# A software-pipelined attention pass: maxima ahead of statistics, the normalised stream a step later, POOL's sums in another order

## The chip, the core and the metric

The kernel runs on one core of a Trainium2 chip. A core has a matrix engine (PE), a vector engine (DVE), an activation engine (ACT), a general engine (POOL) and a queue engine (SP) that issues DMAs. Each engine works through its own instructions in order, and waits on semaphores for the others. PE writes to PSUM, eight banks of 128 partitions by 512 floats; DVE and ACT read them. The metric is the time of one execution on the device in microseconds; lower is better.

## What is computed

A batch of 16 images of 64 x 64 positions with 128 channels goes through a two-dimensional recurrence, an attention layer and a one-dimensional recurrence, each added to its input. The change is in the attention layer, which takes the result as 16 sequences of 4096 tokens. Its core, cut to what matters here (8 heads of 16 channels, 64 landmarks):

```
xn = (x - mu) * rsqrt(var + eps) * gamma + beta
q, k, v = split(xn @ w_qkv);  q = q * dh ** -0.5
q_l, k_l = means of q and k over 64 stretches of the sequence
attn1 = softmax(q   @ k_l^T)        # 4096 x 64 per head
attn2 = softmax(q_l @ k_l^T)        # 64 x 64, inverted by iteration
attn3 = softmax(q_l @ k^T)          # 64 x 4096
out = attn1 @ pinv(attn2) @ (attn3 @ v) + conv(v)
x + out @ w_out + b_out
```

What follows it begins with a layer norm of each token and a product with W, whose mean and variance over all tokens are needed: "the normalised stream" below.

## The kernel before

Earlier stages leave the landmarks and the inverses of attn2 in memory. The attention pass then walks over groups of 512 tokens: Q = 8 groups per image, 128 groups in all, and one call of `step(s)` per group. The work on one group is spread over many steps, so that a step handles several groups at once. In the names of `step`, `new` is the group whose q, k and v are projected; `mid`, one image behind, is weighed by attn3 (`weigh`, `weights`, `attend_values`); `first` and `cur`, nearly two images behind, take attn1: `compare` makes the scores, `topmost` reduces them to maxima, `soften` and `softened` make the exponentials, `attend`, `convolve`, `divide`, `add_convolved` and `turn_attended` the output; `third` projects the output and adds the input (`output`, `keep_sum`, which writes at_u and sends it to memory in two DMAs); `fourth` takes the statistics of at_u and its normalisation. `after` is the next group to be transposed. With `start` (q = 0) a step also closes one image: `gather` normalises the sums of attn3 @ v, `turn_split` prepares the shift of the next image's exponentials, `spread_values` applies the inverse.

The order in which every engine meets its instructions is the order in which `step` calls these helpers; it is written out by hand (`tc.manual_schedule`), and nothing reorders it. SP's DMAs follow the same order. `first_step` serves the first 8 steps, `last_step` those after the last group was projected.

PSUM is the scarce thing. The banks 0 to 5 and a pair of two are used several times in a step, and a matmul into a bank waits until the last reader of its former contents is through. Those that matter here:

- bank 5: second block of `compare`'s scores, read by `topmost` (L1088, tile at_cmx), then `project_queries` (L948), then `weigh`;
- banks 0 to 3: keys and values, then `greatest` (L973), the scores of attn3 over the group, read by `keep_greatest` (L977, four reductions on DVE, bank 3 first), then `output` (L1158, bank 3), `turn_top` (L1104, bank 2) and `turn_output` (L909 on at_z, bank 1);
- bank 2 in a start step: `gather` (L1061, L1063), read by DVE's reciprocal and products (L1066, L1069), before `greatest` uses it;
- bank 3 again: `turn_split` (L956) ahead of `greatest` in a start step, and `feed` (L1189).

On DVE the statistics are `measure` (four bn_stats of at_u with their four aggregates, L1170 and L1171) and `measure_feed` (one bn_stats of at_fx, L1197). On ACT `normalise` makes at_z in four pieces (L1183), `keep_output` copies its transpose (L924), `keep_feed` copies the product (L1193) and sends it to memory by one DMA (L1194). On POOL `add_weights` adds the four chunks of the exponentials at_e into at_total (L1042, L1045; three in their own step, the one of chunk 2 at the front of the next), `factors` makes the scale and bias for `normalise` (L32, L33, L1177, L1178), `carry` and `carry_bias` prepare the residual at_T (L899, L903; on ACT L897), `part_top` splits the maxima into bfloat16 parts (L1096 to L1099) and `shift` the image's maxima (L984 to L991, after a reduction on DVE, L982).

Of the kernel before, what the change touches and what calls it, by code (L numbers as in the profile page):

```python
# [796 lines left out]
def attention(nc, tc, t1, gamma, beta, wqkv, ident, mhalf, fixed, xp, rows, qm, km, pinvT, vd, t2, wx, wx_stats, out):  # L797
# [20 lines left out]
    with ExitStack() as ctx:  # L818
# [86 lines left out]
        def turn(a, k):  # L905

            p = bank(k, [P, C, P])
            for c in range(C):
                nc.tensor.transpose(p[:, c, :], a[:, c, :], ident)  # L909
            return p.rearrange("p c n -> p (c n)")  # L910

        def turn_rows(gr):
            gr.px = turn(gr.xh, 4)

        def keep_rows(gr):
            gr.xT = wk.tile([P, GC], F32, tag="xT", name="at_xT", bufs=2)
# [121 lines left out]
        def add_weights(gr, cs, start=False, eng=nc.gpsimd):  # L1038

            e, total = gr.e, gr.im.total  # L1040
            if start:
                eng.tensor_tensor(total, e[:, :, cs[0], :], e[:, :, cs[1], :], ALU.add)  # L1042
                cs = cs[2:]
            for c in cs:
                eng.tensor_tensor(total, total, e[:, :, c, :], ALU.add)  # L1045
# [73 lines left out]
        def softened(gr):  # L1119
            gr.eT = wk.tile([P, NP, GC], F32, tag="eT", name="at_eT")  # L1120
            for n in range(NP):
                nc.scalar.activation(gr.eT[:, n], gr.s[n], AF.Exp)  # L1122
# [78 lines left out]
        def group(s):  # L1201
            b, g = divmod(s, Q)
            return images[b].groups[g] if b in images else None
# [13 lines left out]
        def first_step(s):  # L1217
            new, after = group(s), group(s + 1)
            both = pair()
            project_keys(new, both[:, 0])  # L1220
            project_values(new, both[:, 1])
            keep_keys(new)
            turn_rows(after)
            keep_projected(new)
            project_queries(new)
            keep_rows(after)
            keep_queries(new)
            greatest(new)
            keep_greatest(new)
            if s == Q - 1:  # L1230
                shift(new.im)
            fetch(s)

        def last_step(s):
            b, q = divmod(s, Q)
            mid, was = group(s - Q), group(s - Q - 1)
            first, cur, third, fourth, fifth = (group(s - 2 * Q + d) for d in (1, 0, -1, -2, -3))
            start = q == 0
            if first:
                compare(first)  # L1240
            if cur:
                softened(cur)
            if start and mid:
                fifth = None
                add_weights(was, (2,))
                sums(mid.im)
                measure(fourth)
                factors(fourth)
                turn_split(mid.im)
            if first:  # L1250
                topmost(first)
                carry_factors(first)
                carry(first, 2, nc.gpsimd)
            if start and was:
                gather(was.im)
            if first:
                part_top(first)
                carry(first, 3, nc.gpsimd)
            if third:
                output(third, 0)  # L1260
                keep_sum(third)
                measure(third)
            if fifth:
                feed(fifth, 1)
                keep_feed(fifth)
                measure_feed(fifth)
            if start and was:
                spread_values(was.im)
            if mid:
                weigh(mid)  # L1270
                weights(mid)
            if fourth:
                normalise(fourth)
            if cur:
                attend(cur)
            if mid:
                add_weights(mid, (3, 1, 0), mid.g == 0)
            if cur:
                convolve(cur, pair())
                divide(cur)  # L1280
            if first:
                turn_top(first)
                keep_top(first)
            if cur:
                add_convolved(cur)
            if mid:
                attend_values(mid)
                keep_values(mid)
            if fourth:
                turn_output(fourth, 4)  # L1290
                keep_output(fourth)
            if first:
                carry(first, 0, nc.scalar)
                carry(first, 1, nc.scalar)
                soften(first)
            if third:
                factors(third)
            if first:
                carry_bias(first)
            if cur:  # L1300
                turn_attended(cur)
            if mid:
                add_weights(mid, (2,), eng=nc.vector)
            fetch(s)

        def step(s):
            b, q = divmod(s, Q)
            new, after, mid, was = group(s), group(s + 1), group(s - Q), group(s - Q - 1)
            first, cur, third, fourth = (group(s - 2 * Q + d) for d in (1, 0, -1, -2))
            start = q == 0  # L1310
            if first:
                compare(first)
            if cur:
                softened(cur)
            if fourth:
                measure(fourth)
            if new:
                project_keys(new)
            if was:
                add_weights(was, (2,))  # L1320
            if start and mid:
                sums(mid.im)
            if new:
                project_values(new)
            if first:
                topmost(first)
            if fourth:
                factors(fourth)
            if new:
                keep_keys(new)  # L1330
                project_queries(new)
                keep_projected(new)
            if start and was:
                gather(was.im)
            if start and mid:
                turn_split(mid.im)
            if new:
                keep_queries(new)
                greatest(new)
            if first:  # L1340
                carry_factors(first)
                carry(first, 2, nc.gpsimd)
            if fourth:
                normalise(fourth)
            if mid:
                weigh(mid)
            if new:
                keep_greatest(new)
            if first:
                part_top(first)  # L1350
            if third:
                output(third)
            if mid:
                weights(mid)
            if first:
                carry(first, 3, nc.gpsimd)
            if new and q == Q - 1:
                shift(new.im)
            if start and was:
                spread_values(was.im)  # L1360
            if first:
                turn_top(first)
            if fourth:
                turn_output(fourth)
            if third:
                keep_sum(third)
            if cur:
                attend(cur)
            if fourth:
                keep_output(fourth)  # L1370
            if mid:
                add_weights(mid, (3, 1, 0), mid.g == 0)
            if cur:
                convolve(cur, pair())
                divide(cur)
            if first:
                carry(first, 0, nc.scalar)
            if fourth:
                feed(fourth)
            if first:  # L1380
                keep_top(first)
            if after:
                turn_rows(after)
            if fourth:
                keep_feed(fourth)
            if after:
                keep_rows(after)
            if cur:
                add_convolved(cur)
            if mid:  # L1390
                attend_values(mid)
                keep_values(mid)
            if first:
                soften(first)
                carry(first, 1, nc.scalar)
                carry_bias(first)
            if cur:
                turn_attended(cur)
            if fourth:
                measure_feed(fourth)  # L1400
            fetch(s)

        with tc.manual_schedule(
            engines={mybir.EngineType.PE, mybir.EngineType.DVE, mybir.EngineType.Activation, mybir.EngineType.Pool}
        ):
            projected(images[0])
            for g, a in enumerate(rows):
                group(g).xh = a
            turn_rows(group(0))
            keep_rows(group(0))  # L1410
            for s in range(Q * (B + 2) + 3):
                (first_step if s < Q else step if s < Q * B else last_step)(s)
# [299 lines left out]
```

## Time and profile before

| | us |
|---|---|
| median of 3 runs | 3751.4 |
| lowest, highest run | 3747.28, 3753.3 |
| the profiled execution | 3744.15 |
| its span | 3742.7 |
| attention steps, first matmul of L928 to the last one's | 1630.43 to 3251.24 |

| engine | busy us | share of the span | instructions |
|---|---|---|---|
| PE | 3519.9 | 94% | 36666 |
| DVE | 3004.0 | 80% | 6991 |
| ACT | 2498.4 | 67% | 5124 |
| POOL | 2520.4 | 67% | 3847 |

Busy shares are averages over stages with different limits, and a matmul's end in the profile is modelled, so a busy PE may still be losing time. The distance between the starts of the same line in successive steps says what a step takes. The steps of the first image (L928 starts 4.32 us apart) only project; those of the second (8.27 apart) also weigh; from the third image on every part runs.

### The profile page before, as it was taken

To read this page: it belongs to the slowest core of one execution; us is meant where nothing else is said; L and a number is where in the kernel's file an instruction comes from. 1 tells how busy PE (TensorE), PEld (TensorE's weight loads), DVE (VectorE), ACT (ScalarE), POOL (GpSimd) and SP (SyncE) were. 2 spreads that over 40 slices of the span, in tenths; PEclk is the share of its full clock that TensorE was granted. 3 is DMA by queue.
4 is the path that set the end of the run, shared out by engine and by line. 5 is a ranking of instruction groups with operands and counts; after the bars stand their busy time and mean duration, and the time that the engine had idled before them with its cause. 6 is when DMAs were issued, how large, how long until landed. Compare 5 with 4: busy or idle time off the path is not lost.

```text
span 3742.7 us, 98455 instructions
## 1 busy us (share of the span) xinstructions
PE 3519.9 (94%) x36666; PEld 2374.7 (63%) x36666; DVE 3004.0 (80%) x6991; ACT 2498.4 (67%) x5124; POOL 2520.4 (67%) x3847
## 2 busy tenths in 40 slices
PE   6899999999999987999999999999999999986897
PEld 5666665545567666965666666666666666653576
DVE  7799999998889886444888888888888888887564
ACT  0466556666667664445777777777777777775796
POOL 0577877777888784426777777777777777783133
PEclk8899999999999997999999999999999999998898
DMA  9223232333333220043666666666666666655999
GB/s 328 82 76 80 80 84 80 85 84 84 85 88 89 78 70 14 5 111 73 160 161 158 159 155 156 157 160 160 161 160 159 154 157 156 149 133 138 269 270 166
DMA packets 834179, 484.01 MB, mean 129 GB/s; under 512 B 304672, under 2 KB 800672, under 8 KB 833696
## 3 DMA queue, kind: packets, MB, share of 16 engines
q1 hardware_dynamic: 811178, 441.43, 45.9%
q0 software_dynamic: 17728, 34.61, 5.2%
q8 instruction: 293, 4.80, 0.6%
q10 hardware_dynamic: 4790, 1.62, 0.2%
q14 instruction: 190, 1.56, 0.1%
HBM read 239.21 MB, written 238.29 MB: 128 GB/s over the span
## 4 chain that ended last, share of the span: by engine, by line
PE 59%; DVE 25%; POOL 5%; issue 4%; ACT 3%; DMA 3%; ACTq 0%; DVEq 0%; SPq 0%; POOLq 0%
PE ls_z L252 13%; PE ls_z L257 13%; PE at_bank L973 4%; DVE at_t L1139 4%; PE lm_bank L541 4%; PE at_bank L948 4%; PE at_bank L1129 3%; PE at_bank L1158 3%; PE at_bank L1009 2%; DVE at_cmx L1088 2%; PE rc_z L1504 2%; DVE at_st L1170 2%; DVE at_m L1143 2%; DVE at_m L1149 2%; POOL at_total L1045 2%
## 5 line engine op out<-in xcount | busy, mean ns | idle before, releaser
L1045 POOL TENSOR_TENSOR at_total<-at_total,at_e 128x512 f32<-128x512 f32 x472 | 635.9, 1347 | 190.1 <-ACT at_e L1018 170.7
L259 ACT ACTIVATE ls_g<-ls_z,ls_b 128x304 f32<-128x304 f32 (+26 forms) x950 | 496.1, 545 | 229.4 <-PE ls_z L257 194.9
L252 PE MATMUL ls_z<-ls_xn,ls_w 128*128 128x432 f32 (+28 forms) x1700 | 591.4, 496 | 3.3 <-POOL ls_xn L244 3.0
L252 PEld LDWEIGHTS ls_z<-ls_xn,ls_w 128*128 128x128 f32 x1700 | 313.1, 193 | 192.6 <-issue 98.7
L977 DVE TENSOR_REDUCE at_mxq<-at_bank 128x1 f32<-128x512 f32 x512 | 317.8, 683 | 128.2 <-PE at_bank L973 128.2
L257 PE MATMUL ls_z<-ls_hsum,ls_u 128*128 128x304 f32 (+26 forms) x1140 | 373.0, 465 | 0.0
L287 POOL TENSOR_TENSOR ls_tt<-ls_ve,mhalf 128x8 f32<-128x8 f32 (+2 forms) x190 | 314.3, 1654 | 15.8
L1122 ACT ACTIVATE at_eT<-at_bank 128x512 f32<-128x512 f32 x512 | 264.0, 602 | 79.5 <-PE at_bank L1117 79.5
L257 PEld LDWEIGHTS ls_z<-ls_hsum,ls_u 128*128 128x128 f32 x1140 | 215.0, 198 | 128.6 <-issue 78.2
L257 PE MATMUL ls_z<-ls_h,ls_u 128*128 128x304 f32 (+26 forms) x760 | 260.8, 467 | 24.7 <-DVE ls_h L374 24.7
L370 ACT ACTIVATE ls_g<-ls_cell 128x304 f32<-128x304 f32 (+26 forms) x190 | 93.2, 491 | 264.1 <-DVE ls_cell L369 260.4
L366 POOL TENSOR_TENSOR ls_g<-ls_g,ls_cell 128x304 f32<-128x304 f32 (+26 forms) x190 | 179.2, 943 | 131.3 <-ACT ls_g L259 112.1
L304 ACT ACTIVATE ls_tt<-ls_tt,ls_nb 128x128 f32<-128x128 f32 (+9 forms) x632 | 261.1, 479 | 4.1 <-POOL ls_nb L299 4.1
L244 POOL TENSOR_TENSOR ls_xn<-ls_xn,grstd 128x304 f32<-128x304 f32 (+26 forms) x190 | 211.2, 1113 | 72.3 <-DVE ls_xn L241 69.2
L1139 DVE STREAM_TRANSPOSE at_t<-at_bank 128x512 f32<-128x512 f32 x256 | 168.2, 695 | 113.8 <-PE at_bank L1129 113.6
L1517 DVE SCALAR_TENSOR_TENSOR rc_y<-rc_w,rc_scale,rc_z 128x256 f32<-128x256 f32 x344 | 155.3, 480 | 108.5 <-PE rc_z L1504 108.2
L1504 PE MATMUL rc_z<-rc_y,rc_vT 128*128 128x256 f32 x688 | 187.7, 409 | 40.2 <-ACT rc_y L1525 28.7
L257 PEld LDWEIGHTS ls_z<-ls_h,ls_u 128*128 128x128 f32 x760 | 143.4, 197 | 118.4 <-issue 53.1
L1193 ACT COPY at_fx<-at_bank 128x512 f32<-128x512 f32 x128 | 133.2, 1041 | 121.0 <-PE at_bank L1189 121.0
L1183 ACT ACTIVATE at_z<-at_u,at_nb,at_r 128x128 f32<-128x128 f32 x512 | 209.4, 483 | 0.0
L1498 POOL DMA_DIRECT2D out_dram<-rc_tt x64 | 77.4, 1209 | 189.5 <-ACT rc_tt L1495 187.6
L903 POOL TENSOR_TENSOR at_T<-at_T,at_bo 128x512 f32<-128x512 f32 x128 | 162.9, 1273 | 51.2 <-ACT at_T L897 51.2
(262 smaller groups left out, 9792.1 us busy)
## 6 DMA issues: line engine op xcount, KB each, us to landing
at_win<-vd SPq DMA_DIRECT2D x256, 256.0 KB
t<-ls_tt SPq DMA_DIRECT2D x392, 130.0 KB
at_T<-t SPq DMA_DIRECT2D x128, 264.0 KB
gs_xb<-in_x_dram SPq DMA_DIRECT2D x64, 512.0 KB
at_xh<-t SPq DMA_DIRECT2D x128, 256.0 KB
vd<-at_v SPq DMA_DIRECT2D x128, 256.0 KB
t<-at_u SPq DMA_DIRECT2D x128, 256.0 KB
out_dram<-at_u SPq DMA_DIRECT2D x128, 256.0 KB
```

Of the source, the lines that this page charges most:

```text
L244: nc.gpsimd.tensor_tensor(a, a, norm(v, grstd), ALU.mult)
L252: nc.tensor.matmul(v.z[g][:, : v.total], wt[g], v.xn[:, : v.total], start=True, stop=True)
L257: nc.tensor.matmul(view(v, v.first.z[g]), ut[g], hin, start=False, stop=True, skip_group_check=True)
L259: nc.scalar.activation(a[:, : v.cols], z, AF.Tanh if g == 4 else AF.Sigmoid, bias=bt[g])
L287: nc.gpsimd.tensor_tensor(v.tt[:, 0:k, F + 2 : F + 4], ve[:, :, :k].rearrange("p r k -> p k r"), mhalf[:, : 2 * k].rearrange("p (k r) -> p ...
L304: nc.scalar.activation(v.tt[:q, k, F + 4 :], v.tt[:q, k, 0:F], AF.Identity, bias=v.nb[:q, k : k + 1], scale=v.tt[:q, k, F + 3 : F + 4],)
L977: nc.vector.tensor_reduce(gr.im.mxq[:, n : n + 1, gr.g], gr.s[n], AX.X, ALU.max)
L1045: eng.tensor_tensor(total, total, e[:, :, c, :], ALU.add)
L1122: nc.scalar.activation(gr.eT[:, n], gr.s[n], AF.Exp)
L1139: nc.vector.transpose(t[:, j].rearrange("p k t d -> p (k t d)"), gr.o[j])
L1183: nc.scalar.activation(gr.z[:, c, :], gr.u[:, c, :], AF.Identity, bias=gr.nb[:, c : c + 1], scale=gr.r3[:, c : c + 1])
L1504: nc.tensor.matmul(gr.z, vT, gr.last, start=True, stop=True)
```

## The change

In `step`, the calls are put in another order, and two groups further back get names, `fifth` and `sixth`:

- `topmost(first)` comes ahead of all statistics of the step. `measure_feed` moves from the end of a step to the place behind `topmost` in the next one (it is now `sixth`), and `measure(fourth)` behind that. So DVE's order from the last work on at_m on is: maxima, bn_stats of at_fx, statistics of at_u, in a start step the reciprocal and products of `gather`, and then the reductions of `keep_greatest`.
- `normalise`, `turn_output`, `keep_output`, `feed` and `keep_feed` work on `fifth`: one step later than before. `factors(fourth)` moves behind the second `carry` on POOL.
- `add_weights` takes all four chunks in its own step; the separate call for chunk 2 at the front of the next step is gone. `shift` comes behind it instead of ahead of it.
- `keep_queries` comes ahead of `turn_split`, `keep_top` ahead of `add_weights`, `carry(first, 0, nc.scalar)` behind `keep_rows`; `project_queries` and `keep_projected` swap places, which are on different engines.
- In `last_step`, the step that follows the last `step` takes over what is now still open: the bn_stats of one group more, `normalise`, `turn_output` and `keep_output` of `fifth`, whose `feed` then follows in the same step; the leftover addition of chunk 2 is gone there.
- `turn_rows` gets a parameter whose value is 4 everywhere, as before. Tests that are always true in `step` are dropped.

Number, shape and engine of the instructions stay the same.

```diff
--- before.py
+++ after.py
@@ -909,8 +909,8 @@
                 nc.tensor.transpose(p[:, c, :], a[:, c, :], ident)
             return p.rearrange("p c n -> p (c n)")
 
-        def turn_rows(gr):
-            gr.px = turn(gr.xh, 4)
+        def turn_rows(gr, k=4):
+            gr.px = turn(gr.xh, k)
 
         def keep_rows(gr):
             gr.xT = wk.tile([P, GC], F32, tag="xT", name="at_xT", bufs=2)
@@ -1220,7 +1220,7 @@
             project_keys(new, both[:, 0])
             project_values(new, both[:, 1])
             keep_keys(new)
-            turn_rows(after)
+            turn_rows(after, 4)
             keep_projected(new)
             project_queries(new)
             keep_rows(after)
@@ -1241,8 +1241,10 @@
             if cur:
                 softened(cur)
             if start and mid:
-                fifth = None
-                add_weights(was, (2,))
+                measure_feed(group(s - 2 * Q - 4))
+                normalise(fifth)
+                turn_output(fifth)
+                keep_output(fifth)
                 sums(mid.im)
                 measure(fourth)
                 factors(fourth)
@@ -1306,98 +1308,86 @@
         def step(s):
             b, q = divmod(s, Q)
             new, after, mid, was = group(s), group(s + 1), group(s - Q), group(s - Q - 1)
-            first, cur, third, fourth = (group(s - 2 * Q + d) for d in (1, 0, -1, -2))
+            first, cur, third, fourth, fifth, sixth = (group(s - 2 * Q + d) for d in (1, 0, -1, -2, -3, -4))
             start = q == 0
             if first:
                 compare(first)
             if cur:
                 softened(cur)
+            project_keys(new)
+            if start:
+                sums(mid.im)
+            project_values(new)
+            if first:
+                topmost(first)
+            if sixth:
+                measure_feed(sixth)
             if fourth:
                 measure(fourth)
-            if new:
-                project_keys(new)
-            if was:
-                add_weights(was, (2,))
-            if start and mid:
-                sums(mid.im)
-            if new:
-                project_values(new)
-            if first:
-                topmost(first)
-            if fourth:
-                factors(fourth)
-            if new:
-                keep_keys(new)
-                project_queries(new)
-                keep_projected(new)
+            keep_keys(new)
+            keep_projected(new)
+            project_queries(new)
             if start and was:
                 gather(was.im)
-            if start and mid:
+            keep_queries(new)
+            if start:
                 turn_split(mid.im)
-            if new:
-                keep_queries(new)
-                greatest(new)
+            if fifth:
+                normalise(fifth)
+            greatest(new)
             if first:
                 carry_factors(first)
                 carry(first, 2, nc.gpsimd)
-            if fourth:
-                normalise(fourth)
-            if mid:
-                weigh(mid)
-            if new:
-                keep_greatest(new)
+            weigh(mid)
+            keep_greatest(new)
             if first:
                 part_top(first)
             if third:
                 output(third)
-            if mid:
-                weights(mid)
+            weights(mid)
             if first:
                 carry(first, 3, nc.gpsimd)
-            if new and q == Q - 1:
-                shift(new.im)
+            if fourth:
+                factors(fourth)
             if start and was:
                 spread_values(was.im)
             if first:
                 turn_top(first)
-            if fourth:
-                turn_output(fourth)
+            if fifth:
+                turn_output(fifth)
+                keep_output(fifth)
             if third:
                 keep_sum(third)
             if cur:
                 attend(cur)
-            if fourth:
-                keep_output(fourth)
-            if mid:
-                add_weights(mid, (3, 1, 0), mid.g == 0)
+            if first:
+                keep_top(first)
+            add_weights(mid, (3, 1, 0, 2), mid.g == 0)
+            if q == Q - 1:
+                shift(new.im)
             if cur:
                 convolve(cur, pair())
                 divide(cur)
+            if fifth:
+                feed(fifth)
+            if after:
+                turn_rows(after)
+            if fifth:
+                keep_feed(fifth)
+            if after:
+                keep_rows(after)
             if first:
                 carry(first, 0, nc.scalar)
-            if fourth:
-                feed(fourth)
-            if first:
-                keep_top(first)
-            if after:
-                turn_rows(after)
-            if fourth:
-                keep_feed(fourth)
-            if after:
-                keep_rows(after)
+            attend_values(mid)
             if cur:
                 add_convolved(cur)
-            if mid:
-                attend_values(mid)
-                keep_values(mid)
+            keep_values(mid)
             if first:
                 soften(first)
                 carry(first, 1, nc.scalar)
                 carry_bias(first)
             if cur:
                 turn_attended(cur)
-            if fourth:
-                measure_feed(fourth)
             fetch(s)
 
         with tc.manual_schedule(
@@ -1406,7 +1396,7 @@
             projected(images[0])
             for g, a in enumerate(rows):
                 group(g).xh = a
-            turn_rows(group(0))
+            turn_rows(group(0), 4)
             keep_rows(group(0))
             for s in range(Q * (B + 2) + 3):
                 (first_step if s < Q else step if s < Q * B else last_step)(s)
```

## The prediction

> **What bounds the kernel now.** I read the share of each engine first, then the chain that ended last, then the times at which the matmuls of line 928 start, one per step, then PE and DVE in order of time over single steps. The matmuls of line 928 show the attention pass to be periodic: from 1850 to 3250 us each image takes a start step of 16.27 us, one of 13.09 and six of 13.20. The question is what sets the 13.20.
>
> ```profile
> PE 59%; DVE 25%; POOL 5%; issue 4%; ACT 3%; DMA 3%; ACTq 0%; DVEq 0%; SPq 0%; POOLq 0%
> ```
>
> PE and DVE take turns on the chain; POOL and ACT are nearly absent. Two steps side by side (columns: stretch, its length, then busy time and count of PE, PEld, DVE, ACT, POOL, then clock, DMA share, GB/s):
>
> ```profile
> 1772.11:1784.88 12.77, 12.77 (x189) 8.54 (x186) 11.01 (x23) 10.12 (x21) 10.59 (x18) 1.00 0.69 152
> ...
> 2545.73:2558.93 13.20, 13.04 (x191) 8.62 (x187) 11.40 (x25) 10.64 (x22) 10.42 (x18) 1.00 0.68 161
> ```
>
> The first is an early step in which DVE has no bn_stats of at_fx yet, but PE has all of its work: PE is busy throughout and the step takes 12.77. That is PE's own length of a step. PE's timeline of that step and of a regular one (start, duration, line):
>
> ```profile
> 1772.11 1.12 PE L928 MATMUL at_bank<-at_xT,wqkv 128*128 128x512 f32 x2
> 1773.07 1.05 PE L938 MATMUL at_bank<-wqkv,at_xT 128*128 128x128 f32 x8
> 1773.96 1.02 PE L948 MATMUL at_bank<-at_xT,wqkv 128*128 128x512 f32 x2
> 1774.92 1.14 PE L973 MATMUL at_bank<-at_KT,qm 32*128 32x512 f32 x8
> ...
> 1777.10 1.16 PE L1158 MATMUL at_bank<-at_wo,at_oT 128*128 128x128 f32 x8
> ...
> 1784.88 1.13 PE L928 MATMUL at_bank<-at_xT,wqkv 128*128 128x512 f32 x2
> ...
> 2532.51 1.13 PE L928 MATMUL at_bank<-at_xT,wqkv 128*128 128x512 f32 x2
> 2533.47 1.05 PE L938 MATMUL at_bank<-wqkv,at_xT 128*128 128x128 f32 x8
> 2534.70 1.13 PE L948 MATMUL at_bank<-at_xT,wqkv 128*128 128x512 f32 x2 [0.17 <-DVE at_cmx L1088]
> 2535.76 1.14 PE L973 MATMUL at_bank<-at_KT,qm 32*128 32x512 f32 x8
> ```
>
> Counted from line 928, an undisturbed step starts L948 at 1.85, L973 at 2.81, L1158 at 4.99 and the next L928 at 12.77. A regular step starts L948 at 2.19 (0.34 late, waiting for the first at_cmx reduction to free bank 5) and L973 1.06 after it, not 0.96: 0.10 more is lost in restarting after the stall. 0.34 + 0.10 is all of the 13.20 - 12.77. DVE is late there because the statistics stand in front of the maxima:
>
> ```profile
> 1759.67 0.69 DVE L1088 TENSOR_REDUCE at_cmx<-at_bank 128x8 f32<-128x512 f32 x1 [0.95 <-PE at_pair L1080]
> ...
> 2544.95 0.65 DVE L1197 BATCH_NORM_STATS2 wx_stats<-at_fx 128x6 f32<-128x512 f32 x1
> 2545.52 0.27 DVE L1170 BATCH_NORM_STATS2 at_st<-at_u 128x6 f32<-128x128 f32 x1
> ...
> 2547.18 0.67 DVE L1088 TENSOR_REDUCE at_cmx<-at_bank 128x8 f32<-128x512 f32 x1
> ...
> 2550.17 2.48 DVE L977 TENSOR_REDUCE at_mxq<-at_bank 128x1 f32<-128x512 f32 x4 [0.59 <-PE at_bank L973]
> ```
>
> From 2544.95 to 2545.52 is one bn_stats of at_fx (0.57), from there to 2547.18 the four pairs of statistics of at_u (1.66).
>
> **The change, part by part.**
>
> Maxima first, in a regular step. The wait of L948 goes: with DVE free, the first maximum starts 0.19 after L928 (1759.67 against 1759.48, the one step where DVE waits for PE at this place with both of the waits it has later) and ends at 0.87, before 1.85. What is late next? The 0.57 + 1.66 of statistics do not leave DVE; they now stand between the maxima and the four reductions of L977, and the first of those frees bank 3, into which L1158 writes (in the program the first matmul of L1158 waits for that very reduction). Before, those reductions waited 0.59 for PE, so they had slack there but not 2.23. Step by step from L928: maxima 0.19 + 2.33 (starts 2547.18 and 2548.89, then 0.60 until DVE takes the next) = 2.52; bn_stats of at_fx to 3.09; statistics of at_u to 4.75; L977 for bank 3, 0.68, to 5.43; handover to PE 0.06 (at_cmx ends 2534.64, L948 starts 2534.70) = 5.49. PE wants L1158 at 4.99: a stall of 0.50 takes the place of one of 0.34. From L1158 to the next L928 PE needs 7.78 (1777.10 to 1784.88), and a restart again 0.10: 5.49 + 7.78 + 0.10 = **13.37 against 13.20**. Bounds: the earliest maximum after a compare is at 0.10 (1729.00 against 1728.90, before that instruction waits for POOL too), the statistics once took 1.59, and the restart may cost nothing: 5.33 + 7.78 = 13.11; the upper end is 13.37 itself. I take the upper end, since its rows are those of the steady form. Behind the late L1158 nothing else gets tight: L977 frees banks 2 and 1 0.60 apart, at 6.07 and 6.67, and L1104 and L909 come at 6.58 and 6.81.
>
> The step after a start step, 13.09 now, becomes 13.37 like the others. Start step: here gather's reciprocal and two products (L1066, L1069) also move behind the statistics. They free bank 2, for which L973's third block waits, and the chain through L1003 and L1009 to L1158 hangs on it:
>
> ```profile
> 2507.46 0.18 DVE L1066 RECIPROCAL at_rs<-at_bank 128x4 f32<-128x4 f32 x1 [0.39 <-PE at_bank L1063]
> 2507.68 0.46 DVE L1069 TENSOR_TENSOR at_av<-at_bank,at_rs 64x64 f32<-64x64 f32 x2
> ...
> 2510.45 1.16 PE L1158 MATMUL at_bank<-at_wo,at_oT 128*128 128x128 f32 x8
> ```
>
> The reciprocal starts 4.30 after L928 (2503.16) now, waiting for PE; after the change at 4.75, waiting for its own queue. L1158 comes 2.31 after the products end, that is L973's 2.18 and a handover, so nothing takes up the 0.45: the start step becomes 16.72. Bounds +0.29 (with 4.59) to +0.45.
>
> The normalised stream one step later. It is 4 activations at_z, 4 transposes, the copy at_zT, L1189 with 2 matmuls, the copy at_fx with one DMA to wx, and one bn_stats. Each step has the same number of each; ACT has 0.69 idle before at_eT in a regular step, at_z already runs straight after at_QT, and the DMA keeps its place in SP's queue between the writes of at_u and the loads. Cost nothing. If that cover were gone, at_z's 1.63 would come before at_e. keep_queries ahead of the cast of the split takes 0.27 off at_QT in a start step; the chain through bank 2 hides it. topT one ACT place earlier and T's carry later fill the same 0.69 (0.49 of it).
>
> POOL's order. The third add moves to the others (4 x 1.43 from the end of at_e at 7.27, to 13.0, then L903 to 14.3, 0.9 into the next step), and the factors (1.7) move into the 1.70 that POOL waits for at_e. at_top is wanted at 6.58 and stands at 4; the factors are wanted a step later. Nothing in a regular step. In the very first start step it pays: PE waits 1.83 for at_total and L956 starts at 1744.98; with adds before the split it can start when seven small POOL operations are through, about 1743.8. That is 1.1; at full clock another 3.2 follow (chain L956, 0.23 + 2.18, at_e and at_g 2.2, L1104 at 1748.5 instead of 1752.12; then 6.64 as in the step from 1765.47 instead of 7.36). PE's clock is granted at 0.60 and 0.50 from 1745 to 1755, after that idle stretch; I do not know if 0.9 of idle does the same, so -1.1 to -4.3, taken as -3.
>
> The Trainium skill ("TensorE: Matmul & The Clock Gate", Part 1, What's actually happening) has the gate halve the clock only after an idle window of about 3.4 us; the row here shows it after 1.83. By the page the shorter wait would keep full clock and this term would be -4.3.
>
> The ends. Without the bn_stats the step at 1784.88 falls back to 12.77, -0.4. The first step of the tail (3251.24 on) takes over one more normalise, transpose and feed at its front: between 0.5 and 3 (L909 and L1189 are 1.5 at full clock, 3 at the 0.50 of 3270 to 3275), taken as +2.
>
> Sum: 82 regular steps x 0.17 = 13.9; 13 steps after a start x 0.28 = 3.6; 13 starts x 0.45 = 5.9; ends -3 - 0.4 + 2 = -1.4. Together **+22 us**. The profiled execution took 3744.15 (span 3742.7 and 1.45 around it), so 3766; the three runs shown have a median of 3751.4, 7 above it, so **3773**.
>
> **The rivals.**
>
> *It goes even.* All three bounds lie low: 82 x -0.09 = -7.4, 13 x 0.02, 13 x 0.29 = 3.8, ends -5: -8, so 3743 to 3758, centre 3750. For it: one step shows 0.10 for the first handover. Against: that instruction had one wait less there.
>
> *It gets faster.* If L1158 did not wait, PE's 12.77 would rule: 82 x -0.43 - 13 x 0.32 = -39, 3711 with the ends. This decides once DVE's chain to bank 3 is under 4.99, that is with 0.50 less of statistics than 2.23. The step at 1772.11, with L1158 at 4.99 and only the maxima and reductions in line, speaks for it; the rows of statistics, 2.23 in every steady step, against.
>
> *POOL becomes the bound.* Adds took 1.6 where they met DVE (3248.46); four at that price end 0.9 later and, with the split, 1.9 more once an image. at_top has 2.5 of slack, so it decides only beyond that; some 2 per start, 3800.
>
> **How the numbers follow.** The forecast 0.63 (own range 3759 to 3780), even 0.22, faster 0.10, POOL 0.05. The range is 3744 to 3781: it holds the forecast and most of the even case. A measurement of this kernel tells about 0.2%, 7.5 us, from no change. Slower by more 0.66, within 0.21, faster 0.13 (the even case spills a little to both sides).
>
> **What would show it.** L948 with no wait 1.85 after L928; a wait of PE at L1158 for L977 of about 0.5; DVE's idle before L977 gone and an idle of about 0.8 before the maxima instead; start steps near 16.7, regular ones near 13.4, L1063 without its 1.83. A regular step below 13.1, or no wait at L1158, proves me wrong.

## The result: slower by 2.7%, with the profile after

| | before | after |
|---|---|---|
| median, us | 3750.38 (6 runs) | 3851.12 (6 runs) |
| lowest to highest | 3747.28 to 3753.3 | 3845.65 to 3856.34 |
| profiled span | 3742.7 | 3854.9 |
| 94 regular steps, together | 1241.3 (13.20 each) | 1315.8 (14.00 each) |
| 13 start steps, together | 211.9 (16.27 each, one 16.64) | 250.9 (16.72 to 21.11) |
| the first start step | 20.24 | 16.32 |

The ratio is 1.0269, 95% interval 1.0256 to 1.0282. Steps are measured from one start of L928 to the next; the 94 and 13 are all from the fourth step behind the first start step on. There the two spans part by 74.5 and 39.0 us, 113.5 in all; the rest of the execution makes up -1.3 (3.8 more ahead of the attention steps, where the code is the same, 3.9 less in the attention steps up to there, 1.2 less at the end).

The chain that ended last breaks off at the last instruction in this profile (POOL, L1488) and says nothing, so the step is read from the timelines. PE in a regular step of the changed kernel (start, duration, line; in brackets the idle time and what ended it):

```profile
2636.54 1.13 PE L928 MATMUL at_bank<-at_xT,wqkv 128*128 128x512 f32 x2
...
2638.39 1.02 PE L948 MATMUL at_bank<-at_xT,wqkv 128*128 128x512 f32 x2
2639.34 1.14 PE L973 MATMUL at_bank<-at_KT,qm 32*128 32x512 f32 x8
...
2642.01 1.16 PE L1158 MATMUL at_bank<-at_wo,at_oT 128*128 128x128 f32 x8 [0.42 <-DVE at_mxq L977]
...
2648.90 0.38 PE L1080 MATMUL at_bank<-km,at_QT 32*128 32x128 f32 x2
2649.44 0.37 PE L1080 MATMUL at_bank<-km,at_QT 32*128 32x128 f32 x1 [0.16 <-DVE at_sums L1036]
...
2650.54 1.13 PE L928 MATMUL at_bank<-at_xT,wqkv 128*128 128x512 f32 x2
```

L948 starts 1.85 after L928, as early as PE can. L1158 comes at 5.47 and waits for L977. Up to here the step is the one forecast. The second stall is not: the first matmuls of L1080 (`compare`) start at 2648.90, the rest only at 2649.44, because bank 5 is still being read by L1036. From L1117 to the next L928 PE needed 1.85 before (2530.66 to 2532.51); here it takes 2.50 (2648.04 to 2650.54). DVE and POOL in that step:

```profile
2636.70 0.69 DVE L1088 TENSOR_REDUCE at_cmx<-at_bank 128x8 f32<-128x512 f32 x1 [0.70 <-PE at_pair L1080]
...
2641.30 2.45 DVE L977 TENSOR_REDUCE at_mxq<-at_bank 128x1 f32<-128x512 f32 x4
2643.67 0.68 DVE L1162 TENSOR_TENSOR at_u<-at_bank,at_T 128x512 f32<-128x512 f32 x1
2645.04 1.32 DVE L1139 STREAM_TRANSPOSE at_t<-at_bank 128x512 f32<-128x512 f32 x2 [0.69 <-PE at_bank L1129]
2646.39 0.35 DVE L1141 RECIPROCAL at_r<-at_t 128x32 f32<-128x32 f32 x1
2646.78 1.62 DVE L1143 TENSOR_TENSOR at_m<-at_t,at_r 128x512 f32<-128x512 f32 x1
2648.50 0.69 DVE L1149 TENSOR_TENSOR at_m<-at_pair,at_m 128x512 f32<-128x512 f32 x1
2649.11 0.28 DVE L1036 TENSOR_TENSOR at_sums<-at_bank,at_sums 128x128 f32<-128x128 f32 x1
```

```profile
2643.84 5.68 POOL L1045 TENSOR_TENSOR at_total<-at_total,at_e 128x512 f32<-128x512 f32 x4 [0.41 <-ACT at_e L1018]
```

L1143 is a product of two operands in SBUF (`divide`). It takes 1.62 here. Over seven steps (minimum, median and maximum in ns), before and after:

```profile
L1143 DVE TENSOR_TENSOR at_m<-at_t,at_r x7: 793/803/869, 2529.4 to 2608.6; 128x512 f32<-128x512 f32 x7
```

```profile
L1143 DVE TENSOR_TENSOR at_m<-at_t,at_r x7: 1601/1612/1616, 2590.8 to 2674.8; 128x512 f32<-128x512 f32 x7
```

The four additions of L1045 run singly at 2643.84, 2645.21, 2646.56 and 2647.92; the third ends at 2647.84. L1143 starts 0.22 after the third has begun and ends 0.55 after the third has ended. The fourth then takes 1.60 where the others take 1.27 to 1.29. The same two in the regular step of before at 2558.93:

```profile
2569.01 0.80 DVE L1143 TENSOR_TENSOR at_m<-at_t,at_r 128x512 f32<-128x512 f32 x1
```

```profile
2566.64 4.31 POOL L1045 TENSOR_TENSOR at_total<-at_total,at_e 128x512 f32<-128x512 f32 x3 [1.70 <-ACT at_e L1018]
```

There L1143 started 0.25 ahead of the end of the second addition (2569.26) and ended at 2569.81: again 0.55 after an addition's end. What changed is which addition it meets, and how much of that addition is left.

The Trainium skill has the reason in "SBUF — State Buffer", Who interferes with whom: a DVE instruction with two SBUF inputs contends with a GpSimd instruction that reads SBUF, over a pair of ports that is an exclusive lock, and the order of issue decides which one waits. The two spans above agree with it, except that L1143 needs 0.55 after the addition's end and not the whole 0.69 that it takes alone (first experiment).

The start steps have a second loss. One at full clock and one not, whole, and the latter in part (columns: stretch, length, busy time and count of PE, PEld, DVE, ACT, POOL, then granted clock, DMA share, GB/s):

```profile
2559.49:2580.55 21.06, 20.20 (x216) 13.56 (x213) 12.12 (x27) 10.70 (x23) 10.44 (x21) 0.76 0.49 119
2678.53:2695.25 16.72, 15.69 (x215) 10.89 (x212) 12.13 (x27) 10.61 (x23) 10.47 (x21) 1.00 0.60 147
...
2565.00:2570.00 5.00, 4.96 (x48) 4.48 (x48) 2.48 (x4) 2.34 (x5) 1.21 (x3) 0.62 0.00 0
2570.00:2575.00 5.00, 4.69 (x56) 2.75 (x56) 0.82 (x2) 1.29 (x3) 3.81 (x3) 0.50 0.57 148
```

The step at full clock takes 16.72. In the other the same work runs for 10.24 us (2566.17 to 2576.41) at half the clock. Eleven of the 13 start steps have such a stretch, of 3.41 or 10.24 us; before, none had.

### The profile page after: what moved, and what is told of

The parts are those of the page before. It is cut to its first block, busy times and chain, and to the rows that moved or that the text cites. A ratio compares the mean times of both kernels' runs of the same rounds, so it can differ in the third digit from the quotient of the medians.

```text
span 3854.9 us, 98547 instructions
## 1 busy us (share of the span) xinstructions
PE 3584.8 (93%) x36666; PEld 2397.6 (62%) x36666; DVE 3081.2 (80%) x6991; ACT 2522.6 (65%) x5124; POOL 2531.0 (66%) x3847
## 3 DMA queue, kind: packets, MB, share of 16 engines
q10 hardware_dynamic: 4790, 1.62, 0.2%
## 5 line engine op out<-in xcount | busy, mean ns | idle before, releaser
L1045 POOL TENSOR_TENSOR at_total<-at_total,at_e 128x512 f32<-128x512 f32 x472 | 637.2, 1350 | 99.4 <-ACT at_e L1018 70.9
L977 DVE TENSOR_REDUCE at_mxq<-at_bank 128x1 f32<-128x512 f32 x512 | 314.8, 677 | 72.9 <-PE at_bank L973 72.9
L1088 DVE TENSOR_REDUCE at_cmx<-at_bank 128x8 f32<-128x512 f32 x256 | 175.8, 687 | 88.6 <-PE at_pair L1080 85.7
L1080 PEld LDWEIGHTS at_bank<-km,at_QT 32*128 32x128 f32 x2048 | 164.1, 186 | 93.3 <-issue 54.6
```

The lines of the kernel that those rows point to most:

```text
L977: nc.vector.tensor_reduce(gr.im.mxq[:, n : n + 1, gr.g], gr.s[n], AX.X, ALU.max)
```

## The experiments

Theory A: late statistics push L1143 from the end of POOL's second addition into its third, and its delay stalls `compare`. Theory D, on the start steps: their own new wait for `gather`'s products brings the low clock. The rivals stand in the expectations.

**Additions taken away.** One operation per image is kept; the sums of the exponentials are left out.

```diff
-            add_weights(mid, (3, 1, 0, 2), mid.g == 0)
+            if mid.g == 0:
+                add_weights(mid, (3, 1), True)
```

> The changed kernel with POOL's additions of at_e left out, but for one operation per image that starts at_total (so the sums of attn3 are not computed; everything else is). In the changed kernel a regular step takes 14.00 us, at_m (L1143) 1.62 us instead of 0.81, and PE stalls twice: 0.48 before L1158 (first reduction of L977) and 0.66 before the matmuls of L1080. Theory A (the second stall is the two-input product at_m held up until POOL's running addition has ended): with no additions at_m takes 0.69, the stall before L1080 goes, the one before L1158 stays; a regular step takes 13.3 to 13.4, the whole some 60 us less, about 3790 if the start steps keep their slow clock. Theory B (the second stall is only DVE's chain being pushed back by the late L1158, whatever POOL does): at_m may shorten, but regular steps stay above 13.8 and the whole above 3835.

3782.56 us (one run). The regular step is 13.37, and L1143 takes:

```profile
L1143 DVE TENSOR_TENSOR at_m<-at_t,at_r x7: 691/692/692, 2591.8 to 2675.3; 128x512 f32<-128x512 f32 x7
```

Alone it takes 0.69, and 13.37 is the length that the prediction gave the step. Seven start steps took 16.71, six 18.16 to 21.08.

**Statistics ahead of the maxima again.**

```diff
+            if sixth:
+                measure_feed(sixth)
+            if fourth:
+                measure(fourth)
             project_keys(new)
 ...
                 topmost(first)
-            if sixth:
-                measure_feed(sixth)
-            if fourth:
-                measure(fourth)
```

> The changed kernel with both groups of statistics put ahead of the maxima again; POOL's order and the later normalised stream stay. Theory A (the place of the statistics on DVE is what costs, first by the stall before L1158, then by the place at which at_m meets POOL's additions, and in the start steps by the reciprocal): regular steps 13.2 again, at_m 0.8, start steps 16.3 at full clock, the first start step about 16.3 instead of 20.2; the whole 3742 to 3752. Rival C (the four additions in one row, or the stream a step later, cost by themselves): regular steps above 13.5 and the whole above 3790.

3742.27 us, ratio 0.9987 to before (0.9977 to 0.9996). The regular step is 13.21 and the start step 16.22 to 16.51, with no low clock, while the first start step stays at 16.33. So the loss hangs on the place of the statistics; the later stream and POOL's order by themselves cost nothing.

**POOL's factors between the additions,** so that L1143 falls among small operations.

```diff
-            if fourth:
-                factors(fourth)
 ...
-            add_weights(mid, (3, 1, 0, 2), mid.g == 0)
+            cs = (3, 1, 0, 2)
+            k = 2 if mid.g == 0 else 1
+            add_weights(mid, cs[:k], mid.g == 0)
+            if fourth:
+                factors(fourth)
+            add_weights(mid, cs[k:])
```

> The changed kernel with factors (POOL, 1.7 us of small operations) moved from ahead of the additions to between the first and the other three: no work less, only another operation of POOL at the place where at_m starts, 2.9 us after the first addition. Theory A: at_m takes 0.7 to 1.0, the stall before L1080 goes, the one before L1158 stays; regular steps 13.3 to 13.4, the whole 3785 to 3800. Theory B: regular steps stay 13.8 to 14.0, the whole above 3835. Start steps: no view; their clock may stay low.

3785.97 us, ratio 1.0100 (1.0083 to 1.0116). POOL and DVE:

```profile
2592.69 1.29 POOL L1045 TENSOR_TENSOR at_total<-at_total,at_e 128x512 f32<-128x512 f32 x1 [2.03 <-ACT at_e L1018]
2594.37 1.04 POOL L33 TENSOR_TENSOR at_r<-at_ve,mhalf 128x4 f32<-128x4 f32 x1
...
2596.39 3.97 POOL L1045 TENSOR_TENSOR at_total<-at_total,at_e 128x512 f32<-128x512 f32 x3
```

```profile
L1143 DVE TENSOR_TENSOR at_m<-at_t,at_r x7: 691/692/692, 2582.3 to 2670.2; 128x512 f32<-128x512 f32 x7
```

All the additions are done, and in the regular steps none runs while L1143 does. It takes 0.69, the regular step 13.37, and the 94 regular steps sum to 1257.3 (1257.6 without the additions). The start steps took 17.12 to 17.40 at full clock, and five had a low one (18.95 to 21.13). That splits the 74.5 of the regular steps: 1257.3 - 1241.3 = 16.0 for the stall at L1158, 1315.8 - 1257.3 = 58.5 for L1143's meeting with an addition.

**Chunk 2 back at the front of the next step.** The third addition is there in either order; is the moved one to blame?

```diff
             project_keys(new)
+            if was:
+                add_weights(was, (2,))
 ...
-            add_weights(mid, (3, 1, 0, 2), mid.g == 0)
+            add_weights(mid, (3, 1, 0), mid.g == 0)
```

The leftover addition in `last_step` is back too.

> The changed kernel with the addition of chunk 2 put back to the front of the next step, as it stood before the change; everything else as changed. Theory (the late product at_m meets the third addition of its own step, which is there in either order, so the moved addition is not to blame): L1143 again at about 1.6 us in a regular step, the regular step 14.00, the run 3840 to 3856. Rival (the fourth addition, or its place, is what holds at_m up): L1143 at 0.69 to 0.81, the regular step 13.37, the run 3775 to 3800.

3853.32 us, ratio 1.0281 (1.0264 to 1.0298). L1143 takes 1.60 to 1.62 in seven steps looked at and the regular step 14.00, so the fourth addition is not to blame. The first start step is 20.55 again, against 16.32.

**Statistics split:** two pairs ahead of L977, two behind it (`measure` takes the pairs as a parameter); the factors go behind the additions.

```diff
             if fourth:
-                measure(fourth)
+                measure(fourth, (0, 1))
 ...
             keep_greatest(new)
+            if fourth:
+                measure(fourth, (2, 3))
 ...
-            if fourth:
-                factors(fourth)
 ...
             add_weights(mid, (3, 1, 0, 2), mid.g == 0)
+            if fourth:
+                factors(fourth)
```

> The changed kernel with two of the four pairs of statistics of at_u moved behind the reductions of L977, and factors behind the additions. Between the maxima and L977 there are then 1.4 us instead of 2.23, so by the chain in the prediction bank 3 is free at 4.7 after L928 and PE wants it at 4.99. Theory A: no stall before L1158 and none before L948, regular steps 12.8 to 13.0, start steps at most 16.3 and no low clock in them, the whole 3700 to 3720, faster than both kernels. Against it: if the two pairs behind L977 delay at_t or put at_m against an addition, regular steps 13.2 to 13.6 and the whole 3745 to 3790.

3706.23 us, ratio 0.9889 (0.9872 to 0.9905): faster than both kernels. A regular step (columns as in the start steps above):

```profile
2541.86:2554.66 12.80, 12.80 (x191) 8.46 (x187) 11.42 (x24) 10.67 (x22) 10.49 (x18) 1.00 0.72 167
```

PE is busy throughout, and most regular steps take 12.77 to 12.79, its own length of a step. L977 starts 4.02 after L928 and L1158 at its 4.99. The start steps take 16.03 (one 16.31), none with a low clock. Four of the 94 steps take 13.96 to 13.98. DVE in one of them, which starts at 2634.62:

```profile
2642.37 0.69 DVE L1162 TENSOR_TENSOR at_u<-at_bank,at_T 128x512 f32<-128x512 f32 x1 [0.45 <-ACT at_zT L924]
...
2644.70 1.73 DVE L1143 TENSOR_TENSOR at_m<-at_t,at_r 128x512 f32<-128x512 f32 x1
```

L1143 comes 10.08 after L928, not 9.74 as in the step at 2541.86, and so 0.09 after the third addition (2644.61) instead of 0.26 ahead of it (2551.60 against 2551.86). It takes 1.73 instead of 0.73, and the step is 1.17 longer. A delay of 0.34 decides. Why L1162 was late there is open: the copy L924 named in brackets is not it, since in the step at 2541.86 L1162 starts (2549.27) before L924 ends (2549.55). It is not chance either, for the same four steps of the pass are long in the reverse run below (13.95 to 13.97).

**Start steps with the statistics and factors behind,** regular steps as changed.

```diff
-            if sixth:
+            if sixth and not start:
                 measure_feed(sixth)
-            if fourth:
+            if fourth and not start:
                 measure(fourth)
 ...
             keep_greatest(new)
+            if sixth and start:
+                measure_feed(sixth)
+            if fourth and start:
+                measure(fourth)
 ...
             add_weights(mid, (3, 1, 0, 2), mid.g == 0)
+            if fourth and start:
+                factors(fourth)
```

The factors stay in their changed place only in a step that is no start step.

> The changed kernel, in which start steps alone take the statistics behind the reductions of L977 and factors behind the additions; regular steps are as in the changed kernel. There the 13 start steps take 16.72 us at full clock (two of them) and up to 21.11 where the clock is granted at 0.50 for some 8 us (eleven); in a start step PE stalls 0.55 before L973's third block and 0.47 before L1104. Theory D (the idle of the start step itself brings the low clock): without the stall before L973 no start step is slow, all take 15.9 to 16.3, regular steps stay at 14.00, the whole 3805 to 3815. Theory E (the two stalls of every regular step before it have already lowered PE's share of busy time, and that brings the low clock): several start steps stay at 18 to 21, the whole above 3825.

3818.66 us, ratio 1.0187 (1.0170 to 1.0204); the whole a little above what was expected. One start step:

```profile
2540.97:2557.11 16.14, 15.36 (x216) 10.89 (x213) 12.14 (x27) 10.60 (x23) 10.67 (x21) 1.00 0.47 114
```

All 13 take 16.14 at full clock, while the regular steps remain at 14.00 with both stalls. So the stalls of regular steps do not bring the low clock into the start step.

**The reverse:** the split everywhere but in start steps.

```diff
-                measure(fourth, (0, 1))
+                measure(fourth, (0, 1, 2, 3) if start else (0, 1))
 ...
-            if fourth:
+            if fourth and not start:
                 measure(fourth, (2, 3))
```

(The diff is against the split kernel.)

> The kernel with split statistics (regular steps 12.79 with PE never stalled, start steps 16.03), in which start steps alone take all statistics ahead of gather's reciprocal, as in the changed kernel. At full clock a start step is then 16.6 to 16.8 by the chain of the prediction (reciprocal at 4.75 instead of about 4). Theory D: the stall before L973 is back, and several of the 13 start steps go to 18 to 21 although no regular step stalls; the whole 3718 to 3745. Theory E: no start step is slow, all 16.6 to 16.8, the whole 3712 to 3718.

3727.6 us, ratio 0.9953 (0.9936 to 0.9970). Two of its start steps:

```profile
2489.89:2506.60 16.71, 15.84 (x217) 10.95 (x213) 12.13 (x27) 11.16 (x24) 13.00 (x29) 1.00 0.68 157
2596.11:2617.20 21.09, 20.36 (x217) 13.70 (x213) 12.12 (x27) 11.26 (x24) 13.11 (x29) 0.76 0.54 125
```

Regular steps are 12.79, yet five start steps have a low clock (18.16 to 21.13). So the order in the start step itself brings it, and theory D holds from both sides. But the wait is not the one of 0.55 before L973 that was expected back. In the slower of the two:

```profile
2600.31 0.33 PE L956 MATMUL at_bank<-ident,at_split 128*128 128x128 f32 x1 [0.42 <-POOL at_split L991]
```

The split kernel waits at the same place, 0.44 in its start step at 2580.24, and keeps its clock in all 13. What the late reciprocal adds is 0.17 inside L973: from its first block to L1003 it is 1.13 (2600.57 to 2601.70) against 0.96 there (2584.72 to 2585.68).

**The changed kernel once more,** unaltered.

> The changed kernel once more, unaltered. In its first profile 11 of the 13 start steps had a low granted clock for part of their length; the two that had not started 1.12 and 2.48 us into a period of 3.413 us, counted from the span's start, the others at 2.68 to 3.11 and 0.06 to 0.45. Theory (a period that runs on by itself decides which start steps are caught): slow and full-speed start steps again lie in one stretch each of that period, but the stretch lies elsewhere and other images are slow. Rival (something in the work of an image decides): the same 11 images are slow, and the 8th and 9th are not. Regular steps 14.00 in both, the run 3820 to 3860.

3849.13 us (one run). The lengths of the start steps, by where they start in a period of 3.4135 us (from the span's start):

```
this run   0.26 16.71 | 0.27 16.71 | 0.40 16.70 | 0.53 18.13 | 0.59 18.13 | 0.67 21.06 | 0.68 21.06
           0.80 21.07 | 0.96 21.05 | 1.11 21.06 | 2.32 16.71 | 2.33 16.71 | 2.44 16.71
first run  0.36 21.11 | 0.99 16.98 | 2.35 16.72 | 2.52 18.14 | 2.57 18.15 | 2.59 18.14 | 2.64 18.14
           2.68 18.15 | 2.77 21.06 | 2.95 21.06 | 3.01 21.07 | 3.33 21.11 | 3.38 21.11
```

In each run the low-clock steps lie in one stretch of the period, 18.1 first and 21.1 behind it. The stretch begins near 0.5 in one and 2.5 in the other. Other images are caught: in this run the 2nd, 3rd, 6th, 7th, 12th and 13th are not, in the first run the 8th and 9th. The rival falls.

## Why the prediction was right in direction and wrong in size

Terms that held:
- L948's wait went (1.85 after L928) and a wait for L977 took its place: L1158 at 5.47, forecast 5.49.
- The regular step without the meeting of L1143 and an addition: 13.37, forecast 13.37. Over the 94 steps this is 16.0 us, forecast 13.9 + 3.6. Part of the agreement is luck. The sum had 0.10 for a restart of PE after the stall, and there is none: L1104 follows L1158 by 0.99, as in a step without the stall. The 0.10 was lost further on, 0.06 of it before L909 on at_z (0.29 behind L1104, else 0.23) and 0.03 before L1129; the reason is open.
- The start step at full clock: 16.70 to 16.72 in the two profiles (one 16.98), forecast 16.72; 13 x 16.71 - 211.9 = 5.3, forecast 5.9.
- The first start step: -3.9, forecast -3. The clock is in this number: the step of 20.24 held 10.24 us of low clock, that of 16.32 held 3.41 us. In the second profile of the changed kernel it held none and took 15.92, and that is the -4.3 that the prediction worked out for full clock. That POOL's order brings the gain is shown by the return to 20.55 with chunk 2 put back. The tail was 1.2 shorter, in the second profile 0.1 longer, and not 2 longer.

Two small errors of the sum: the maxima's 2.33 is 2.31 by the rows named there (with it L1158 is at 5.47, as measured), and the profile has 81 regular steps besides the 13 behind a start step, not 82.

Two steps failed:
- "Behind the late L1158 nothing else gets tight" looked only at PE's banks 2 and 1. The late L1158 delays L1162, the transposes and L1143 too; L1143 moved from 2.37 to 2.94 after the start of the additions and so past the start of the third one, at 2.72. Before, 0.25 of the second addition was left; now most of the third is. Its end comes 0.97 later in the step (11.85 after L928, was 10.88), and L1036, behind it on DVE, then holds bank 5. Price: 58.5 us, more than half of the loss. The prediction saw additions of "1.6 where they met DVE", but priced them for POOL, where they cost nothing, and not for DVE. "Nothing in a regular step" for POOL's order held: the third addition stood there already, and with chunk 2 put back the step is still 14.00.
- The start step was priced at full clock throughout. The 0.45 of delay came true, and with it a low clock in 11 of 13 start steps: 250.9 - 217.2 = 33.7 us in this profile, 24.6 in the second, where seven were caught. The prediction weighed the granted clock only for the first start step.

The sum closes: 16.0 + 58.5 + 5.3 + 33.7 - 1.3 = 112.2, the difference of the spans. Of the rivals, "it gets faster" named the right point (0.50 less statistics ahead of bank 3): the split kernel passed it and its regular step fell to PE's length. The step at 1772.11 that this rival leaned on did hold statistics, those of at_u from 1771.50 to 1773.07; it lacked the one of at_fx alone. POOL did not become the bound.

## What to carry to other kernels

Moving work on one engine moves everything behind it against the other engines' instructions: follow the delayed chain to the end of the step, and look at what each instruction newly runs beside, not only at what it waits for. An instruction that takes 0.69 alone, 0.80 here and 0.87 there may be sharing something; find with whom, and how far it is from the worst meeting, before it is shifted. Where the order must feed a critical reduction, split the block that stands in front of it rather than move the whole block.

## What the hardware showed

**DVE's product waits for POOL's addition.** L1143 took 0.69 alone, 0.73 to 0.87 when it began shortly before the end of an addition, and 1.60 to 1.73 when it began shortly after the start of one. In the steps opened above it ended 0.54 to 0.55 after that addition's end.

**A clock that falls after short stalls, by a period of its own.** In a start step with the low clock no single idle time of PE is long. The start of the one at 2559.49:

```profile
2562.31 0.95 PE L1063 MATMUL at_bank<-at_ones,at_total 128*128 128x2 f32 x8
...
2565.04 0.70 PE L973 MATMUL at_bank<-at_KT,qm 32*128 32x512 f32 x2 [0.55 <-DVE at_av L1069]
...
2568.10 2.08 PE L1158 MATMUL at_bank<-at_wo,at_oT 128*128 128x128 f32 x8
```

The wait before the last blocks of L973 is 0.55, behind eight matmuls of two columns each, and by L1158 the same eight matmuls take 2.08 instead of 1.16. Over the six runs with such steps (the changed kernel twice; no additions; factors between; split but in start steps; chunk 2 put back), every period from 1.5 to 8 us was tried in steps of 0.001: the only one that gathers the low-clock starts of all six into one stretch each is 3.414. 3.413 does it for five, and no other for more than three. The profile's record of the granted clock shows the period directly: in every run here each change of the clock lies within 0.01 us of a grid of 3.4133 us. In the start steps the low clock lasts one such period (3.41 us) or three (10.24), and it begins 5.57 to 6.93 after L928.

The Trainium skill, "TensorE: Matmul & The Clock Gate", Part 1, What's actually happening, gives a free-running window of 3413 ns, which agrees. Its rule that an idle window comes before the lower clock does not cover these rows: here 0.55 of waiting was enough, where a period ended in that stretch of the step.

How little work in a period is too little was not measured, but the rows put it between two cases. In the split kernel nine start steps have a period ending 5.7 to 6.7 after L928, where every start step of the six runs was caught, and with 0.44 of waiting before L956 they keep the clock. In the reverse run 0.42 there and the 0.17 inside L973 lose it. Stalls later in the step, in the run with the start statistics behind 0.47 before L1104 and 0.31 before L1189, brought no low clock.
